# Two attention layers on one core: the first layer's products alternate between the two halves of a query block

## The chip, the cores and the metric

The kernel runs on one core of a Trainium2 chip. The metric is the device time of one execution in microseconds (us). The kernel before took 3090.68 us (median of 3 runs, 3089.88 to 3092.52).

## What is computed

The input x has 4 images of 64 x 64 tokens with 256 channels. Two attention layers follow each other. In the reference, cut to what matters:

```python
q = x @ Wq + bq; k = x @ Wk + bk; v = x @ Wv + bv          # layer 0: q, k have 32 channels, v has 256
attn = softmax(q @ k.T);  x = gamma * (attn @ v) + x       # 4096 queries x 4096 keys in each image
f = x @ Wf + bf; g = x @ Wg + bg; v = x @ Wh + bh          # layer 1: f, g have 32 channels, v has 128
beta = softmax(g @ f.T);  out = x + (beta @ v) @ Wo + bo
```

## The kernel before, in words

Nothing of size 4096 x 4096 is stored. Both layers go through blocks of queries, and within a block through steps over the keys. The first layer has blocks of 256 queries (16 in an image) and steps of 512 keys (8 in a block, each four key tiles of 128); the second has blocks of 512 queries and 16 steps of 256 keys. So each image has 128 steps of the first layer and 128 of the second; the change is in the first, in 4 x 16 = 64 blocks and 512 steps.

A step of the first layer does this:

- Scores: TensorE multiplies four key tiles with the block's queries into a PSUM tile `st` of two banks (line 640, four matmuls of 256 columns; two of them go to one bank, two to the next).
- ScalarE takes two exponentials of `st`: `high` (line 650, with a small negative bias, rounded to fp32r) and `p` (line 657, fp32).
- VectorE cuts the rest into `low` = p - high (line 678) and `d`, a combination of low and high (line 683). With three such forms of p and three of v (`v0h`, `v0l`, `v0d`), three passes of fp32r matmuls stand for one pass of higher precision.
- Products: TensorE multiplies p's forms with v's (line 708). The 128 queries of a half of the block are the stationary operand (a weight load of 128 columns per product), and v's row tile of 256 channels and two extra columns is the moving operand: 258 columns, or 256 for the l form outside a block's last step. A half has two accumulators in PSUM, one for h and l, one for d: `acc0` and `acc1` for the first half, the two banks of `acc_pair` for the second. Each is a bank of its own.

With three forms, four key tiles and two halves a step has 24 products. Call the eight products of one form in one step a section. `products_first` (line 701) issues the four products of one half and one form. The loop over the steps (from line 1039) calls it: in the inner steps of a block the order is h of half 0, h of half 1, l of half 0, l of half 1; in a block's first and last step (`s.first`, `s.last`) it is h and l of half 0, then h and l of half 1. After these come the scores of the step after next (`later.scores()`) and other small work of the plan (`todo`: projections, transposes), and then d of both halves (lines 1134 and 1135).

At a block's end `take_first` (line 744) copies a half's h and l accumulator with ScalarE to a tile `o`, as soon as that half's h and l are done, and `end_first` (line 748) adds the d accumulator with VectorE (line 752), first half first. The rest of the end (reciprocal of the sums, residual, stores) is put into later steps.

The tiles of v are allocated once, one after another (lines 366 to 374): for each of the 8 key steps the forms h, l and d, each with four rows of 260 fp32 numbers per partition (`ROW = C + 4`), 1,040 bytes a row and 4,160 bytes a tile. The forms of p are 128 x 1024 fp32 tiles; key tile g and half s begin at g x 1,024 + s x 512 bytes in a partition.

From step 8 on (`MANUAL_FROM`, line 1044) each engine executes its instructions in the order in which the program issues them. In the first 8 steps, the first block of the first image, the compiler's scheduler decides the order.

Of the kernel before, what the change touches and what calls it, by code (L numbers as in the profile page):

```python
# [57 lines left out]
P = 128  # L58
# [194 lines left out]
def fast_path(ctx: ExitStack, tc: tile.TileContext, x, w0, w1, wo, bo, gamma, out, off):  # L253

    nc = tc.nc
# [8 lines left out]
    G = (4, 2)  # L264
# [101 lines left out]
    v0 = []  # L366
# [190 lines left out]
    def project_stages(b, l, h):  # L557
        return transpose_stages(b, l, h), qk_stages(b, l, h), v_stages(b, l, h)
# [28 lines left out]
    def wide(name, until, dtype=F32):  # L587
        step = now[0] % PER_IMAGE - PER_LAYER
        until_step = until - (now[0] - now[0] % PER_IMAGE) - PER_LAYER

        def may_have(k):
            if isinstance(k, int):
                return True
            if isinstance(k, str):
                return step >= 0 and now[0] // PER_IMAGE == B - 1
            if dtype != F32R or step < 0:
                return False
            return now[0] // PER_IMAGE == B - 1 or until_step < VALUES_FROM[k[0]]

        which = min((k for k in free_at if may_have(k)), key=free_at.get)  # L600
        free_at[which] = until
        while any(held is not None and held == in_slot.get(which) for _, _, _, held in later_sums):
            later_sums.pop(0)[2]()
        in_slot[which] = name
        if isinstance(which, str):
            return const.tile([P, NT, QB0], dtype, tag=which, name=name)
        if not isinstance(which, int):
            return v0[which[0]][which[1]][:, :, :C]
        return work.tile([P, NT, QB0], dtype, tag=f"wide{which}", bufs=1, name=name)

    def small(name):
        return work.tile([P, C], F32, tag="small", bufs=4, name=name)


    class Step:
# [82 lines left out]

            later_sums.append((1.15, self.n + (KEEP if self.n < last_block else 0), issue, f"p_{self.key}"))

        def products_first(self, acc, s, what):
            p, v, which = {
                "h": (self.high, "h", 0), "l": (self.low, "l", 0), "d": (self.d, "d", 1)
            }[what]

            width = C if what == "l" and not self.last else W
            for g in range(G[0]):
                nc.tensor.matmul(  # L708
                    acc[2 * s + which][:, :width],
                    p[:, g, s * P : (s + 1) * P],  # L710
                    v0[self.i][v][:, g, :width],
                    start=self.first and what != "l" and g == 0,
                    stop=self.last and what != "h" and g == G[0] - 1,
                )

        def products_second(self, acc, parts, halves=(slice(0, QB // QB0),), between=None):
            v = v_t[self.b, self.i]
# [22 lines left out]
    def out_rows(b, j, s):  # L740
        row = j * QB0 + s * P
        return out[b, row : row + P, :]

    def take_first(b, j, acc, o, s):
        o.append(work.tile([P, W], F32, tag="o", name=f"o_{b}_{j}_{s}"))
        nc.scalar.activation(o[s], acc[2 * s][:, :W], AF.Copy, scale=1.0 + EPS)
# [175 lines left out]
    def run(stages):  # L922
        for u in stages:
            u()
# [78 lines left out]
    acc, p_sum, o = None, None, []  # L1003
# [35 lines left out]
    for n, s in enumerate(steps):  # L1039
        now[0] = n  # L1040
        b, l, j = s.b, s.l, s.j
        if n == last_block:
            tc.mark_branch_hint_location("in_range", "LikelyTaken", mybir.ALL_ENGINES)
        if n == MANUAL_FROM:
            ordered.enter_context(tc.manual_schedule())
        if s.first:
            o = []
            acc = [ps_main.tile([P, QB], F32, tag=f"acc{a}", name=f"acc{a}_{b}_{l}_{j}") for a in range(2)]
            if l == 0:
                pair = ps_main.tile([P, 2, QB], F32, tag="pair", name=f"acc_pair_{b}_{j}")  # L1050
                acc += [pair[:, a, :] for a in range(2)]
            if l == 1:
                p_sum = wide(f"p_sum_{b}_{j}", n + NI[1] + MOVED_AT + 2.5)
        if l == 0 and s.i == NI[0] - 3:
            x_res[b, j] = []
            for t in range(NS):
                x_res[b, j].append(small(f"x_res_{b}_{j}_{t}"))
                row = (j * NS + t) * P
                nc.sync.dma_start(x_res[b, j][t], x[b, row : row + P, :])
                nc.sync.dma_start(out_rows(b, j, t), bias[1, :].partition_broadcast(P))  # L1060
        if l == 0 and s.i == NI[0] - 2:
            for t in range(NS):
                nc.gpsimd.dma_start(x_res[b, j][t], bias[0, :].partition_broadcast(P), accum_op=ALU.add)

        ahead = steps[n + Q_AHEAD] if n + Q_AHEAD < len(steps) else None
        if ahead is not None and ahead.first:
            k = (ahead.b, ahead.l, ahead.j * (QB0, QB)[ahead.l] // QB)
            if k not in q_t:
                load_q(*k)
        if b == l == j == 0 and s.i == 5:  # L1070
            load_q(0, 0, 0, slice(QB0, QB), qk_dram[0, 0, 0].bitcast(F32R)[:, :, :, QB0:])
        after, later = (steps[n + k] if n + k < len(steps) else beyond for k in (1, 2))

        early = []
        if b == l == j == 0 and s.i + AHEAD < NB:
            early = [project_stages(0, 0, 2 * (s.i + AHEAD) + k) for k in range(2)]
            run([u for x in early for u in x[0]])

        run(todo.pop((n, "a"), []))
        s.move_sum()  # L1080
        if l == 0:
            s.cut_both()
            after.cut_low()
        else:
            cost = 1.9 if s.split else 2.2
            tensor_clock += cost + 1.7 * (b + 1 < B and s.i in (3, 7)) + 0.86 * (j > 0 and s.i in (13, 14))
            vector_clock = max(vector_clock, tensor_clock - cost)
            s.cut_both()
            after.cut_low()
            vector_clock += 1.15 * (s.split + after.split)  # L1090
            if n < len(steps) - 2:
                s.add_up(p_sum)
        if l == 1:
            if n == len(steps) - 2:
                while later_sums:
                    later_sums.pop(0)[2]()
                last_sums(p_sum)
            if s.last:
                o = take_first_two(b, j, acc)
            if s.first and j == 0:  # L1100
                s.products_second(acc, ("h", "l"))
            later.scores()
            run(todo.pop((n, "b"), []))

            while later_sums and (later_sums[0][1] <= n or vector_clock + later_sums[0][0] <= tensor_clock + AHEAD_OF):
                took, _, issue, _ = later_sums.pop(0)
                issue()
                vector_clock += took
            behind = steps[n - 1] if not s.first and steps[n - 1].split else None
            if s.last and behind:  # L1110
                behind.products_second(acc, ("d",))
            if n == len(steps) - 1:
                halves = [slice(k, k + 1) for k in range(QB // QB0)]
                s.products_second(acc, ("whole",), halves, last_denominators)
            elif not (s.first and j == 0):
                s.products_second(acc, ("h", "l") if s.split else ("whole",))
            if not s.last and behind:
                behind.products_second(acc, ("d",))
            if n == len(steps) - 1:
                last_outputs(acc, o)  # L1120
            elif s.last:
                vector_clock += 0.8
                end_second(b, j, acc, p_sum, o, n + 1)
        else:

            for half, what in ((0, "h"), (0, "l"), (1, "h"), (1, "l")) if s.first or s.last else ((0, "h"), (1, "h"), (0, "l"), (1, "l")):
                s.products_first(acc, half, what)
                if s.last and what == "l":
                    take_first(b, j, acc, o, half)
            if early:  # L1130
                run([u for x in early for u in x[1] + x[2]])
            later.scores()
            run(todo.pop((n, "b"), []))
            for half in (0, 1):
                s.products_first(acc, half, "d")
            if s.last:
                end_first(b, j, acc, o, n + 1)

        over = (min(s.i + 2, NI[l] - 1) + 1) * G[l] // NT if j == NQ[l] - 1 else 0
        while keys and stored.get(keys[0], n + 1) <= n and (keys[0][:2] == (b, l) or keys[0][2] < over):  # L1140
            load_k(*keys.pop(0))
# [55 lines left out]
```

## Time and profile before

| what | value |
|---|---|
| median of 3 runs | 3090.68 us |
| the profiled execution's own time | 3090.66 us |
| its span, first to last instruction | 3088.8 us |
| mean granted TensorE clock | 0.999 |
| TensorE busy | 3065.6 us (99%) |
| weight loads busy | 2668.0 us (86%) |
| VectorE busy | 2743.3 us (89%) |
| ScalarE busy | 2198.2 us (71%) |
| products of the first layer (line 708) | 12,288 |

Matmuls are pipelined, so a matmul's own length in the profile (some 280 ns for a product) overlaps its neighbours' and does not say how fast they follow each other; for that one compares the starts. "PEld" is TensorE's weight load, "PEclk" the granted clock in tenths. A line of a group reads: line, engine, operation, output <- inputs, size, count | busy us, mean ns of one | idle time of the engine ahead of it, and what ended most of that. A line of sums over a window reads: window, length, then busy us and number of instructions of TensorE, weight loads, VectorE, ScalarE and GpSimd, then the clock, the DMAs' share and GB/s.

### The profile page before, as it was taken

Reading aid. Unit: us, or ns where it says so; the run is one execution under the profiler, and the core shown is the slowest. Engines: PE = TensorE matmul, PEld = TensorE weight load, DVE = VectorE, ACT = ScalarE, POOL = GpSimd, SP = SyncE. Lnnn points to the kernel's source line nnn. Section 1 sums busy time; section 2 is a strip of 40 time slices with the busy share of each in tenths; the row PEclk is TensorE's granted clock in tenths of the full one; section 3 lists DMA queues with packets and bytes.
Section 4 is the critical chain, followed back from the end, with each engine's and each line's share of the span. In section 5 each row is a group of like instructions: output and inputs, shape, how many; then the busy total and the mean of one; then the engine's idle time right before and its main releaser. Section 6 shows DMA issues by size and latency. Waiting matters only on the chain.

```text
span 3088.8 us, 55044 instructions
## 1 busy us (share of the span) xinstructions
PE 3065.6 (99%) x19908; PEld 2668.0 (86%) x19908; DVE 2743.3 (89%) x3317; ACT 2198.2 (71%) x2900; POOL 788.9 (26%) x1157
## 2 busy tenths in 40 slices
PE   8999999999999999999999999999999999999999
PEld 7999998666799999866689999976668999997666
DVE  7889989999889999999989998999998888888887
ACT  6777777777677777777767677777776666667775
POOL 5111113222421111422241111132234111124332
PEclk9999999999999999999999999999999999999999
DMA  5344445666644444666664444466666333337877
GB/s 134 77 90 88 90 88 116 141 135 136 131 89 90 88 91 88 129 132 136 133 126 94 87 91 88 89 132 130 133 136 118 64 68 74 60 75 159 158 155 144
DMA packets 458888, 338.45 MB, mean 110 GB/s; under 512 B 266386, under 2 KB 400404, under 8 KB 458612
## 3 DMA queue, kind: packets, MB, share of 16 engines
q0 software_dynamic: 112272, 196.49, 35.4%
q1 hardware_dynamic: 345140, 137.80, 18.3%
q8 instruction: 161, 2.64, 0.4%
q14 instruction: 115, 0.94, 0.1%
q10 hardware_dynamic: 1200, 0.59, 0.1%
HBM read 134.74 MB, written 101.78 MB: 77 GB/s over the span
## 4 chain that ended last, share of the span: by engine, by line
PE 91%; DVE 4%; DMA 1%; issue 1%; ACT 1%; SPq 0%; POOL 0%; ACTq 0%; DVEq 0%; POOLq 0%
PE acc_pair L708 23%; PE acc L708 23%; PE acc L732 23%; PE st L640 14%; PE psv L509 5%; PE psqk L458 2%; PE pso L846 2%; DMA p_sum_moved<-p 1%; DVE p_sum L697 1%; DVE d L683 1%; DVE low L678 0%; ACT p L657 0%; SPq L293 0%; DVE v0l L683 0%; DVE v0h L678 0%
## 5 line engine op out<-in xcount | busy, mean ns | idle before, releaser
L650 ACT ACTIVATE high<-st,down 128x1024 fp32r<-128x1024 f32 x651 | 727.3, 1117 | 651.6 <-PE st L640 557.5
L657 ACT ACTIVATE p<-st 128x1024 f32<-128x1024 f32 x1024 | 1023.3, 1019 | 30.7 <-DMA p_sum_moved<-p 16.4
L678 DVE TENSOR_TENSOR low<-p,high 128x1024 fp32r<-128x1024 f32 x565 | 690.5, 1222 | 134.8 <-ACT p L657 130.2
L683 DVE SCALAR_TENSOR_TENSOR d<-low,high 128x1024 fp32r<-128x1024 f32 x547 | 667.5, 1220 | 14.5
L640 PE MATMUL st<-q,k 128*128 128x256 f32 (+1 forms) x3072 | 660.1, 323 | 1.9 <-ACT p L657 1.0
L640 PEld LDWEIGHTS st<-q,k 128*128 128x128 f32 x3072 | 469.0, 188 | 59.6 <-issue 13.0
L732 PE MATMUL acc<-p,v 128*128 128x512 f32 (+1 forms) x1028 | 482.5, 592 | 0.2
L708 PE MATMUL acc<-v0d,d 128*128 128x258 f32 x2048 | 336.7, 286 | 2.2 <-DVE d L683 2.0
L708 PE MATMUL acc_pair<-v0h,high 128*128 128x258 f32 x2048 | 330.2, 283 | 0.0
L708 PE MATMUL acc<-v0h,high 128*128 128x258 f32 x2048 | 330.2, 283 | 0.0
L708 PE MATMUL acc_pair<-v0d,d 128*128 128x258 f32 x2048 | 329.9, 283 | 0.0
L708 PE MATMUL acc_pair<-v0l,low 128*128 128x256 f32 (+1 forms) x2048 | 325.4, 281 | 0.0
L708 PE MATMUL acc<-v0l,low 128*128 128x256 f32 (+1 forms) x2048 | 324.9, 280 | 0.0
L773 POOL DMA_DIRECT2D out<-x x128 | 114.3, 893 | 810.7 <-DVE x L767 795.6
L732 PEld LDWEIGHTS acc<-p,v 128*128 128x128 f32 x1028 | 192.1, 189 | 143.9 <-issue 124.5
L697 DVE TENSOR_TENSOR p_sum<-p_sum,p 128x1024 f32<-128x1024 f32 x239 | 291.3, 1219 | 0.4
L708 PEld LDWEIGHTS acc<-v0d,d 128*128 128x128 f32 x2048 | 282.2, 190 | 4.9 <-DVE d L683 3.7
L671 POOL DMA_DIRECT2D p_sum_moved<-p x167 | 151.8, 913 | 517.1 <-DMA p_sum_moved<-p 196.2
L708 PEld LDWEIGHTS acc<-v0h,high 128*128 128x128 f32 x2048 | 282.4, 190 | 1.5 <-ACT o L789 0.8
L708 PEld LDWEIGHTS acc_pair<-v0h,high 128*128 128x128 f32 x2048 | 281.4, 189 | 0.3 <-DVE o L752 0.2
L708 PEld LDWEIGHTS acc_pair<-v0d,d 128*128 128x128 f32 x2048 | 280.7, 189 | 0.1
L708 PEld LDWEIGHTS acc_pair<-v0l,low 128*128 128x128 f32 x2048 | 277.3, 188 | 0.0
(181 smaller groups left out, 4281.0 us busy)
## 6 DMA issues: line engine op xcount, KB each, us to landing
p_sum_moved<-p POOLq DMA_DIRECT2D x207, 512.0 KB, 4.9
x_res<-in_x SPq DMA_DIRECT2D x128, 128.0 KB, 3.2
qk_dram<-qk_parts SPq DMA_DIRECT2D x128, 128.0 KB, 2.2
x_res<-bias POOLq DMA_DIRECT2D x128, 128.0 KB, 4.1
out<-bias SPq DMA_DIRECT2D x128, 128.0 KB, 4.2
out<-x POOLq DMA_DIRECT2D x128, 128.0 KB, 3.1
q<-qk_dram POOLq DMA_DIRECT2D x252, 64.0 KB, 3.8
out<-y POOLq DMA_DIRECT2D x124, 128.0 KB, 4.0
```

The lines of the kernel that those rows point to most:

```text
L458: nc.tensor.matmul(t["ps"], wqk[l][:, c, :], x_parts[key][n][:, c, :], start=(c == n == 0), stop=(c == NCC - 1 and n == 1),)
L509: nc.tensor.matmul(ps[:, n, :], xT[key][:, c, n * P : (n + 1) * P], wv[l][:, c, :], start=(c == 0), stop=(c == NCC - 1),)
L640: nc.tensor.matmul(st[:, g, :], k_t[b, l, kt // NT][:, kt % NT * P : (kt % NT + 1) * P], q_t[b, l, j * n // QB][:, q0 : q0 + n], start=Tru ...
L650: nc.scalar.activation(self.high, s_flat, AF.Exp, bias=down)
L657: nc.scalar.activation(self.p, s_flat, AF.Exp)
L671: nc.gpsimd.dma_start(moved_sums[b, j, order % both], self.p, accum_op=ALU.add)
L678: nc.vector.tensor_sub(self.low, self.p, self.high.bitcast(F32))
L683: nc.vector.scalar_tensor_tensor(self.d, self.low.bitcast(F32), -UP, self.high.bitcast(F32), ALU.mult, ALU.add)
L697: nc.vector.tensor_add(p_sum, other, self.p)
L708: nc.tensor.matmul(acc[2 * s + which][:, :width], p[:, g, s * P : (s + 1) * P], v0[self.i][v][:, g, :width], start=self.first and what != ...
L732: nc.tensor.matmul(acc[which].rearrange("p (a n) -> p a n", n=QB0)[:, cols, :], v_part[:, g, :], p[:, g * NS : (g + 1) * NS, :][:, cols, : ...
L773: nc.gpsimd.dma_start(out_rows(b, j, s), x_new, accum_op=ALU.add)
```

## The change

`products_first` takes the halves as a list and loops over them inside the loop over the key tiles. In the inner steps of a block h and l are issued for both halves together, so that the products of the two halves alternate for each key tile; d is issued so in all steps. In a block's first and last step h and l keep their order. The line numbers after line 708 grow by one.

```diff
-        def products_first(self, acc, s, what):
+        def products_first(self, acc, halves, what):
...
             for g in range(G[0]):
-                nc.tensor.matmul(
-                    acc[2 * s + which][:, :width],
-                    p[:, g, s * P : (s + 1) * P],
-                    v0[self.i][v][:, g, :width],
-                    start=self.first and what != "l" and g == 0,
-                    stop=self.last and what != "h" and g == G[0] - 1,
-                )
+                for s in halves:
+                    nc.tensor.matmul(
+                        acc[2 * s + which][:, :width],
+                        p[:, g, s * P : (s + 1) * P],
+                        v0[self.i][v][:, g, :width],
+                        start=self.first and what != "l" and g == 0,
+                        stop=self.last and what != "h" and g == G[0] - 1,
+                    )
...
-            for half, what in ((0, "h"), (0, "l"), (1, "h"), (1, "l")) if s.first or s.last else ((0, "h"), (1, "h"), (0, "l"), (1, "l")):
-                s.products_first(acc, half, what)
+            ends = s.first or s.last
+            for halves, what in (((0,), "h"), ((0,), "l"), ((1,), "h"), ((1,), "l")) if ends else (((0, 1), "h"), ((0, 1), "l")):
+                s.products_first(acc, halves, what)
                 if s.last and what == "l":
-                    take_first(b, j, acc, o, half)
+                    take_first(b, j, acc, o, halves[0])
...
-            for half in (0, 1):
-                s.products_first(acc, half, "d")
+            s.products_first(acc, (0, 1), "d")
```

## Prediction, made before the changed kernel ran

> **What bounds the kernel now.** I read the page first (busy times, the clock row, the chain), then the timeline of TensorE over one step of the first layer, then the sums over whole blocks of queries, then the waits of the tile `o`.
>
> ```profile
> PE 3065.6 (99%) x19908; PEld 2668.0 (86%) x19908; DVE 2743.3 (89%) x3317; ACT 2198.2 (71%) x2900; POOL 788.9 (26%) x1157
> ...
> PEclk9999999999999999999999999999999999999999
> ...
> PE acc_pair L708 23%; PE acc L708 23%; PE acc L732 23%; PE st L640 14%; PE psv L509 5%; PE psqk L458 2%; PE pso L846 2%; DMA p_sum_moved<-p 1%; DVE p_sum L697 1%; DVE d L683 1%; DVE low L678 0%; ACT p L657 0%; SPq L293 0%; DVE v0l L683 0%; DVE v0h L678 0%
> ...
> L708 PE MATMUL acc<-v0d,d 128*128 128x258 f32 x2048 | 336.7, 286 | 2.2 <-DVE d L683 2.0
> L708 PE MATMUL acc_pair<-v0h,high 128*128 128x258 f32 x2048 | 330.2, 283 | 0.0
> ```
>
> TensorE is busy 99% at full clock, 46% of the chain is line 708, and those products wait for next to nothing (the idle column: 0.0 to 2.2 us). Three whole blocks (256 queries, 8 key steps each) say it again:
>
> ```profile
> 993.07:1021.59 28.52, 28.52 (x242) 28.52 (x241) 26.14 (x35) 20.21 (x28) 3.48 (x4) 1.00 0.45 84
> 1021.59:1050.11 28.52, 28.52 (x242) 28.52 (x241) 25.48 (x33) 20.20 (x28) 5.55 (x8) 1.00 0.48 96
> 1050.11:1078.63 28.52, 28.52 (x242) 28.52 (x241) 26.14 (x35) 20.20 (x28) 3.48 (x4) 1.00 0.45 84
> ```
>
> Every block takes 28.52 us, whatever VectorE (fourth figure: 26.14 or 25.48 us) and the DMAs do. So the first layer's time is the sum of the distances from one matmul's start to the next one's, and a change of order is worth what it does to these distances. A row's mean (283 ns) is no help: matmuls overlap. One step in the timeline (start, length, engine, line):
>
> ```profile
> 1028.69 0.64 PE L708 MATMUL acc_pair<-v0d,d 128*128 128x258 f32 x4
> 1029.17 0.64 PE L708 MATMUL acc<-v0h,high 128*128 128x258 f32 x4
> 1029.65 0.64 PE L708 MATMUL acc_pair<-v0h,high 128*128 128x258 f32 x4
> 1030.13 0.63 PE L708 MATMUL acc<-v0l,low 128*128 128x256 f32 x4
> 1030.60 0.63 PE L708 MATMUL acc_pair<-v0l,low 128*128 128x256 f32 x4
> 1031.06 0.64 PE L640 MATMUL st<-q,k 128*128 128x256 f32 x4
> ```
>
> From start to start four products take 0.48 us (258 columns) or 0.46 to 0.47 (256): 120 and 117 ns each.
>
> **The change, part by part.** Nothing is added or removed: the same products, weight loads and operands. The built programs' order is the same on ScalarE, GpSimd and SyncE, with every DMA in its place. On TensorE the products of a section (one of h, l, d in one step: 4 key tiles x 2 halves) go 0,1,0,1,... where they went 0,0,0,0,1,1,1,1. That holds for d in all 512 steps (4,096 products) and for h and l in the 6 inner steps of 8 (384 x 16 = 6,144): 10,240 products.
>
> *Distance of one product.* I took the starts of the trace one by one (after 100 us, distances over 140 ns left out). They depend on the place in the block and on hardly anything else: 11,001 distances between products have a variance of 10.0 ns2, of which 1.3 is left once the product's moving operand and the weights loaded next to it are fixed (addresses modulo 2,048). They run from 114 to 130 ns and repeat: at key steps 1 and 5 the third product of h's second half takes 129.9 and 130.0 ns, that of its first half 119.2 and 119.2. These steps' tiles of v are 4 x 3 x 4,160 = 49,920 bytes apart, a multiple of 256. So the place of the moving operand modulo 256 bytes, and what went before, set the distance. Under the change each product keeps its moving operand. The weights loaded beside it are other ones (512 bytes on, not 1,024), but as all these starts differ by multiples of 512 the places modulo 256 stay the same set. If the place decides, the mean stays: 119.2 ns over the 80 places concerned (h and l: 6 steps x 4 key tiles each, d: 8 x 4; 119.0 first half, 119.4 second). Gain or loss: 0.
>
> *Bounds.* At one place the two halves differ, by 3.3 ns on average. If both took the shorter, the mean would fall by 1.63 ns; if the longer, rise by 1.63: 10,240 x 1.63 = 16.7 us either way. Between these I take 0, the row's own mean. The scatter: there are 12 kinds of section (three forms, four places), whose means have a standard deviation of 1.1 ns; a fresh draw of 12 against the old one moves the mean by 1.1 x sqrt(2/12) = 0.46 ns, 4.7 us.
>
> *What the Trainium skill says.* "TensorE: Matmul & The Clock Gate", section "Back-to-back issue gap", gives columns / 2.4 + 2.5 ns: 110.0 ns for 258 columns. By that every order costs the same, the change is worth nothing, and 9 ns of each product are unexplained. The row is 119.2 and varies with the place, so order can matter; the rows decide, and the page is no reason for a narrow range. The same page, "A second HAM failure mode: psum-queue depth-cycling", speaks against the change: cycling through PSUM banks made TensorE fall back to half clock now and then. At 258 / 1.2 = 215 ns, 10,240 products would cost 980 us more. But the scores (L640) change banks every second matmul already, the products every fourth, and the clock is 1.00 in all three blocks: I cost it at 0.
>
> *End of a block.* Here the first half's d sum is complete later: before, four products ahead of the second's, now one, so 3 x 0.12 = 0.36 us later. VectorE adds both to `o` (L752):
>
> ```profile
> 1021.38 0.42 DVE L752 TENSOR_TENSOR o<-o,acc 128x258 f32<-128x258 f32 x1 [1.00 <-PE acc L708]
> ...
> 1021.87 0.42 DVE L752 TENSOR_TENSOR o<-o,acc_pair 128x258 f32<-128x258 f32 x1
> ...
> 1022.21 1.22 DVE L683 SCALAR_TENSOR_TENSOR d<-low,high 128x1024 fp32r<-128x1024 f32 x1
> ...
> 1024.76 0.54 PEld L708 LDWEIGHTS acc<-v0d,d 128*128 128x128 f32 x4
> ```
>
> The first add starts at 1021.74 and the second follows it, 1022.23 instead of 1021.87. Queued behind are L683's d, 0.3 to 0.4 us later (done near 1023.8), and the next low. TensorE wants that d at 1024.76: the 1.34 us between 1023.42 and there shrink to about 1.0. The same 1.34 stands at nearly all of the other ends inside the layer (0.43 at each image's first, once per image). VectorE idles 1.0 us at each end, so the delay doesn't add up. Cost 0; with this cover gone, up to 64 x 0.36 = 23 us. In the four switches to the second layer an add also frees a bank for scores: at most 4 x 0.36 = 1.4 us, taken as 0.
>
> *New waits.* The second half's first d product comes 0.36 us sooner and needs its bank emptied by L752, done at 1022.3 (now 1022.65) against 1024.9. No wait. In the first image's first block end, where the order is not by hand, VectorE now has one d ahead of the two adds; 0.43 us of cover stand against at most 1 us of loss, once. I take 0.
>
> Sum: 3090.66 (the profiled execution: span 3088.8 and 1.9 around it; the median of the runs is 3090.68) + 0 = 3091.
>
> **The rivals.** *Faster: changing accumulators pays.* Distances that lead to the other accumulator average 118.9 ns against 120.2 that stay (258 columns), 116.6 against 118.1 (256): 1.4 ns less. Each section has one such change inside now and would have 7: 6 x 1,280 sections x 1.4 ns = 10.8 us, 3080. Against it: of these changes, those from d to the next h average 120.6, no better than staying; and on the scores, which stay, change, stay, the three distances are 117.7, 117.7 and 119.2. Few places lie behind the 1.4.
>
> *Slower: the repeated read costs.* Two products in a row now read the same v, with weights 512 bytes apart. Only the scores do just that (same q, k tiles 512 bytes apart, 256 columns): 118.2 ns on average against 117.7 for l, +0.5 ns, 5 us. If instead both halves fall into the longer distance of their place, 16.7 us. Between these I price the case at 1 ns, 10 us: 3101. It decides the sign from a mean distance of 119.8 on (0.6 x 10,240 = 6 us). For it: the longest distances (130 ns) are near their worst already in one half only, and a place is now used twice running.
>
> *No effect at all*, the order being undone on the chip: matmuls start in the order written in this trace, so I give it no share apart from the first case.
>
> **How the numbers follow.** No shift, 3091: 0.40. Faster by the accumulators, 3080: 0.26. Slower by the repeated read, 3101: 0.32. Clock or the block's end after all, beyond 3104: 0.02. A measurement tells about 0.2% (6.2 us) from no change. With 4.7 us of scatter the first case gives 0.34 within that and 0.03 on each side; the second 0.22 faster, 0.04 within; the third 0.26 slower, 0.06 within. Faster 0.25, same 0.44, slower 0.31. The range reaches to a little beyond the two rivals' values: 3078 to 3104. The likeliest case's own range is 3085 to 3097.
>
> **What would show it.** A block is 28.52 us: at 0 shift it stays within 0.08; by the first rival it is 28.3, by the second 28.7. Eight alternating products should take 0.96 us from start to start, single distances still between 114 and 130 and repeating with key step + 4. The waits of L752 grow by about 0.36 us each (now 60.0 us in all), with no wait of TensorE for d behind it. I am wrong if the distances leave that band or lose their pattern, if the clock row drops under 9, or if products begin to wait for L683 or L752.

## The result and the profile after

The changed kernel takes 3103.01 us (median of 6 runs, 3099.68 to 3104.70) against 3091.73 us (6 runs, 3089.88 to 3093.51): a ratio of 1.0037, 95% interval 1.0026 to 1.0048. It is slower by 0.4%, some 11.3 us. The profiled execution took 3101.95 us with a span of 3100.2 us; the one of before took 3090.66 us with 3088.8, so the traces differ by 11.4 us of span and stand for the medians.

The page of the kernel after, with the rows that answer to those of before, and the row of one weight load:

```profile
PE 3076.2 (99%) x19908; PEld 2675.6 (86%) x19908; DVE 2735.9 (88%) x3317; ACT 2200.5 (71%) x2900; POOL 791.1 (26%) x1157
...
PEclk9999999999999999999999999999999999999999
...
L709 PE MATMUL acc<-v0d,d 128*128 128x258 f32 x2048 | 518.9, 285 | 1.8 <-DVE d L683 1.7
...
L709 PE MATMUL acc_pair<-v0h,high 128*128 128x258 f32 x2048 | 474.4, 286 | 0.8 <-DVE o L753 0.8
...
L709 PEld LDWEIGHTS acc_pair<-v0h,high 128*128 128x128 f32 x2048 | 361.6, 190 | 4.2 <-DVE o L753 1.2
```

The same weight loads on the page of before:

```profile
L708 PEld LDWEIGHTS acc_pair<-v0h,high 128*128 128x128 f32 x2048 | 281.4, 189 | 0.3 <-DVE o L752 0.2
```

Two traps lie in these rows. First, the busy time of `acc_pair<-v0h` grew from 330.2 to 474.4 us, and no product became that much slower: busy time is the union of overlapping lengths, and products of one group that alternate with another group's overlap each other less. Second, the idle time of these products is 0.8 us, which looks like nothing. What tells more is the releaser named there, `o L753`, and the idle time of the weight loads ahead of them: 0.3 us before, 4.2 us after. The weight loads' row of before names the same releaser already, with 0.2 us.

Sums over three whole blocks (window, length, then busy us and instructions of TensorE, weight loads, VectorE, ScalarE and GpSimd, clock, DMA share, GB/s):

```profile
997.91:1026.56 28.65, 28.65 (x243) 28.60 (x242) 26.00 (x35) 20.23 (x28) 3.49 (x4) 1.00 0.44 84
1026.56:1055.21 28.65, 28.65 (x243) 28.60 (x242) 25.32 (x33) 20.21 (x28) 5.56 (x8) 1.00 0.49 96
1055.21:1083.87 28.66, 28.66 (x243) 28.61 (x242) 25.99 (x35) 20.23 (x28) 3.49 (x4) 1.00 0.43 84
```

A block takes 28.65 us instead of 28.52, again the same in every block, at clock 1.00. That is +0.13 to 0.14 us for each of 64 blocks, 9 us in all. Taken from the starts of the trace, the first layer grew from 1851.70 to 1861.34 us (first to last product of each image, the four summed): 9.64 of the 11.4 us. The weight loads now fill 28.60 us of a window where they filled 28.52 of 28.52: each block has 0.05 us in which none runs. So somewhere in the block something waits. The block's end in the timeline (start, length, engine, line), first before, where the second add to `o` starts at 1021.87 and ends at 1022.29:

```profile
1022.44 0.55 PEld L708 LDWEIGHTS acc_pair<-v0h,high 128*128 128x128 f32 x4
1022.55 0.65 PE L708 MATMUL acc_pair<-v0h,high 128*128 128x258 f32 x4
```

And after:

```profile
1026.56 0.42 DVE L753 TENSOR_TENSOR o<-o,acc 128x258 f32<-128x258 f32 x1 [1.36 <-PE acc L709]
...
1026.90 0.42 DVE L753 TENSOR_TENSOR o<-o,acc_pair 128x258 f32<-128x258 f32 x1
1027.23 1.22 DVE L683 SCALAR_TENSOR_TENSOR d<-low,high 128x1024 fp32r<-128x1024 f32 x1
...
1027.37 0.54 PEld L709 LDWEIGHTS acc_pair<-v0h,high 128*128 128x128 f32 x4
1027.37 0.75 PE L709 MATMUL acc_pair<-v0h,high 128*128 128x258 f32 x4
...
1027.95 0.63 PE L709 MATMUL acc_pair<-v0l,low 128*128 128x256 f32 x4
```

Before, the weights of half 1's first product in the next block are loaded 0.11 us ahead of its start (1022.44, then 1022.55), 0.15 us after the second add has ended. After, the add ends at 1027.32 and the load and the product both start at 1027.37: they were held by it, and the load no longer lies beside the product before. The group of four is 0.75 us long where it was 0.65. The product that follows comes 223 ns after the first instead of 119 (medians over the blocks): 0.104 us a block. A product's modelled length is some 283 ns and covers a distance of 223, so the profile shows almost no idle time of TensorE.

### The profile page after: what moved, and what is told of

Its sections match the earlier page's. It is cut to its first block, busy times and chain, and to the rows that moved or that the text cites. A ratio compares the mean times of both kernels' runs of the same rounds, so it can differ in the third digit from the quotient of the medians.

```text
span 3100.2 us, 55045 instructions
## 1 busy us (share of the span) xinstructions
PE 3076.2 (99%) x19908; PEld 2675.6 (86%) x19908; DVE 2735.9 (88%) x3317; ACT 2200.5 (71%) x2900; POOL 791.1 (26%) x1157
## 4 chain that ended last, share of the span: by engine, by line
PE 93%; DVE 4%; DMA 1%; issue 1%; ACT 1%; SPq 0%; POOL 0%; DVEq 0%; POOLq 0%; ACTq 0%
PE acc L733 23%; PE acc_pair L709 23%; PE acc L709 23%; PE st L640 15%; PE psv L509 5%; PE pso L847 2%; PE psqk L458 2%; DVE p_sum L697 1%; DVE d L683 0%; DVE low L678 0%; DMA p_sum_moved<-p 0%; SPq L293 0%; DVE v0h L678 0%; DVE qk_parts L485 0%; DMA q<-qk_dram 0%
## 5 line engine op out<-in xcount | busy, mean ns | idle before, releaser
L709 PE MATMUL acc<-v0d,d 128*128 128x258 f32 x2048 | 518.9, 285 | 1.8 <-DVE d L683 1.7
L709 PE MATMUL acc_pair<-v0d,d 128*128 128x258 f32 x2048 | 513.0, 283 | 0.0
L709 PE MATMUL acc_pair<-v0h,high 128*128 128x258 f32 x2048 | 474.4, 286 | 0.8 <-DVE o L753 0.8
L709 PE MATMUL acc<-v0h,high 128*128 128x258 f32 x2048 | 469.3, 284 | 0.0
L709 PE MATMUL acc<-v0l,low 128*128 128x256 f32 (+1 forms) x2048 | 463.9, 281 | 0.0
L709 PE MATMUL acc_pair<-v0l,low 128*128 128x256 f32 (+1 forms) x2048 | 462.4, 281 | 0.0
L709 PEld LDWEIGHTS acc<-v0d,d 128*128 128x128 f32 x2048 | 389.4, 190 | 4.0 <-DVE d L683 2.9
L709 PEld LDWEIGHTS acc_pair<-v0d,d 128*128 128x128 f32 x2048 | 387.4, 189 | 0.6
L709 PEld LDWEIGHTS acc<-v0l,low 128*128 128x128 f32 x2048 | 359.6, 189 | 0.0
L709 PEld LDWEIGHTS acc_pair<-v0l,low 128*128 128x128 f32 x2048 | 359.1, 188 | 0.0
```

The source lines that it names most:

```text
L709: nc.tensor.matmul(acc[2 * s + which][:, :width], p[:, g, s * P : (s + 1) * P], v0[self.i][v][:, g, :width], start=self.first and what != ...
```

## The experiments

The theories, as the expectations name them. W: half 1's first h product waits for the second add to `o`, since the two banks of `acc_pair` are one tile, and the alternating d of a block's last step completes half 0 later and so delays both adds. R: the repeated read of the same v costs, wherever products alternate. P: the place of v against the weights in memory decides, and the order only draws other places. Block times are medians over the first three images, from the starts of the one profiled execution of each kernel; before has 28.520 us and after 28.660.

**Only the last step's d as before, or only that changed.** These two split the change in two. The first, on the kernel after:

```diff
-            s.products_first(acc, (0, 1), "d")
+            for halves in (((0,), (1,)) if s.last else ((0, 1),)):
+                s.products_first(acc, halves, "d")
```

> As the changed kernel, but in a block's last step d keeps its old order (half 0, then half 1). Theory W (a wait): two thirds of the loss is a wait at each block's start, where the first h product of half 1 needs the tile acc_pair, which the second add to o frees 0.1 us too late; 61 x 0.104 us and 0.94 us once. Then a block takes 28.55 us instead of 28.65 and the kernel about 3096 us. Theory R (the repeated read of v makes the products slow, and nothing else): 7 of 8 steps still repeat, so about 3102 us and 28.64 us a block.

The second keeps the old order of h, l and d everywhere but for d in a block's last step:

```diff
+            for halves in (((0, 1),) if s.last else ((0,), (1,))):
+                s.products_first(acc, halves, "d")
```

> As the kernel before, but in a block's last step d alternates. Theory W: the whole wait is here: about 28.62 us a block (28.52 + 0.104) and 3099 us. Theory R: only 512 of the 10,240 products repeat: 28.53 us a block and 3092 us, no change.

The weight loads of half 1's h on the page of the first, then on the page of the second:

```profile
L709 PEld LDWEIGHTS acc_pair<-v0h,high 128*128 128x128 f32 x2048 | 362.9, 190 | 0.3 <-DVE o L753 0.2
```

```profile
L709 PEld LDWEIGHTS acc_pair<-v0h,high 128*128 128x128 f32 x2048 | 280.7, 190 | 4.2 <-DVE o L753 1.2
```

The idle time of 4.2 us follows the last step's d alone. With it as before, a block is 28.553 us and the kernel 3093.80 us (before on the same chip 3090.91; 1.0010, 1.0003 to 1.0017). With only it changed, 28.620 us and 3099.32 us (1.0029, 1.0018 to 1.0041). So the 512 products at block ends (eight at each of 64), of 10,240 with a changed place, carry 0.100 us of the block's 0.140; everything else in the change carries 0.033.

**Same order of products, the other add first.** On the kernel after, in `end_first`:

```diff
-        for s in range(NS):
+        for s in reversed(range(NS)):
```

> As the changed kernel, with all its alternation, but VectorE adds half 1 to o first, so that acc_pair is free 0.33 us earlier; acc1 is needed only three microseconds later. Theory W: no wait, 28.55 us a block and about 3096 us. Theory R: as the changed kernel, 28.65 us and 3103 us.

The block's end in its timeline:

```profile
1024.48 0.42 DVE L753 TENSOR_TENSOR o<-o,acc_pair 128x258 f32<-128x258 f32 x1 [1.48 <-PE acc_pair L709]
...
1024.82 0.42 DVE L753 TENSOR_TENSOR o<-o,acc 128x258 f32<-128x258 f32 x1
...
1025.05 0.55 PEld L709 LDWEIGHTS acc_pair<-v0h,high 128*128 128x128 f32 x4
...
1025.16 0.65 PE L709 MATMUL acc_pair<-v0h,high 128*128 128x258 f32 x4
```

Here the add that reads `acc_pair` comes first: VectorE waits 1.48 us for the products that it adds, longer than for the first add after the change, and yet it ends at 1024.90, 0.15 us ahead of the load. The load leads its product by 0.11 us again, the group is 0.65 us long, the distance is 120 ns, and the block takes 28.540 us. TensorE's order is that of the kernel after, so the wait was the add and not the order of products. The first layer takes 7.8 us less than after, 7.4 of them in the distances around half 1's first h product. The kernel takes 3096.48 us, 1.0020 of before (1.0010 to 1.0029) where after took 1.0037. But that is 5.6 us over before, of which the first layer has only 1.85 (1853.55 against 1851.70).

**Alternating without repeating v.** From here on the question is the small rest: what alternating itself does to the distances. On the kernel with the other add first, half 1 takes its key tiles two, one or three further on, so that neighbours no longer read the same v:

```diff
+                    gs = (g + 2 * s) % G[0] if len(halves) > 1 else g
...
-                        p[:, g, s * P : (s + 1) * P],
-                        v0[self.i][v][:, g, :width],
+                        p[:, gs, s * P : (s + 1) * P],
+                        v0[self.i][v][:, gs, :width],
```

> As the kernel that adds half 1 first, but half 1 runs two key tiles behind half 0: the accumulators still alternate, no two products in a row read the same v. Theory R: what the wait does not explain (0.03 to 0.04 us a block) goes: 28.52 us a block and 3092 us. Theory P (the distance of a product is set by the place of its operands, so every order is a fresh draw): the block differs from that kernel's 28.55 us by up to 0.05 us either way, single distances again between 114 and 130 ns.

> Half 1 added to o first, halves alternating, half 1 one key tile ahead: 3 of the 7 steps inside a section read the v of the product just before. Theory R (a repeated read of v costs): 3/4 of the way from the two-tiles-apart kernel (28.493 us a block) to the straight alternation (28.540, where 4 of 7 repeat): about 28.53 us. Theory P (the place decides, each order is a fresh draw): anything from 28.45 to 28.58 us, section by section unlike both.

> The same with half 1 three key tiles ahead: no repeated read of v, accumulators alternate. Theory R: as two tiles apart, 28.49 us a block. Theory P: anything from 28.45 to 28.58 us. If alternating accumulators by itself helped, this one and the last would both lie below the 28.52 us of before.

| order of an alternating section | block, us | first layer, us | span of the profiled execution, us |
|---|---|---|---|
| same tile (v read twice running) | 28.540 | 1853.55 | 3094.3 |
| half 1 two tiles on | 28.493 | 1851.61 | 3090.9 |
| half 1 one tile on | 28.527 | 1854.36 | 3093.6 |
| half 1 three tiles on | 28.560 | 1856.35 | 3094.5 |
| halves in turn (before) | 28.520 | 1851.70 | 3088.8 |

R falls as the cause: three tiles apart reads no v twice running and is the slowest of the four. A cost of the repeated read that is small against the 0.067 us between these orders isn't excluded. That a change of accumulator pays falls too, since all four change it at every product and lie on both sides of before. Two tiles apart was also timed: 3093.74 us against 3090.91 (1.0010, 1.0003 to 1.0017), not faster as a whole although its blocks are.

**Moving the operands in memory, nothing else.** Three kernels on the order of before. In one, v's tiles of the last key step are allocated first, so that each step's v lies where the next step's lay:

```diff
-    v0 = []
-    for j in range(NB):
+    v0 = [None] * NB
+    for j in (NB - 1, *range(NB - 1)):
...
-        v0.append(forms)
+        v0[j] = forms
```

> The kernel before, order of products untouched; the tiles of v of key step 7 are allocated first, so that each step's v lies where the next step's lay. Theory P: a section's time moves along with the place: h of steps 1 to 6 takes 955, 959, 956, 963, 955, 959 ns for its eight products (before 963, 955, 959, 956, 963, 955), l takes 937, 944, 943, 942, 937, 944 (before 942, 937, 944, 943, 942, 937); the block stays within 0.02 us of 28.52. If the position in the block or the order decides instead, the sections keep their times.

In the next a tile of 32 bytes a partition, allocated after v and written once at the start, moves p and all that follows by 32 bytes; in the third the same tile is allocated ahead of v and moves v and p together:

```diff
+    nc.vector.memset(const.tile([P, 8], F32, name="gap"), 0.0)
```

> The kernel before, order untouched, 32 unused bytes a partition allocated after v, so that p's forms lie 32 bytes further on against v. Theory P: a fresh draw at the same set of places: sections change by up to 20 ns each, the block stays within 0.1 us of 28.52. If the operands' places don't matter, sections and block are those of before (28.52).

> The kernel before, order untouched, 32 unused bytes a partition allocated ahead of v, so that v and p both lie 32 bytes further on. If only the place of v against the weights counts, sections and block are those of before: h 963, 955, 959, 956, 963, 955 ns, 28.52 us. If the place of v by itself counts, they change by up to 20 ns a section, as when p alone was moved.

Time from the start of one section of h to the start of the next section, eight products, in ns (medians):

| kernel | step 1 | step 2 | step 3 | step 4 | step 5 | step 6 |
|---|---|---|---|---|---|---|
| before | 963 | 955 | 959 | 956 | 963 | 955 |
| v one step on | 955 | 959 | 952 | 963 | 955 | 959 |
| p 32 bytes on | 958 | 953 | 967 | 964 | 958 | 953 |
| v and p 32 bytes on | 963 | 955 | 959 | 952 | 963 | 955 |
| after (alternating) | 967 | 973 | 951 | 959 | 956 | 973 |

With v one step on, the row of before moves one step to the left, within 4 ns. With p alone 32 bytes on, four of the six sections change by 5 to 8 ns and the other two by 2. With both moved, the row of before comes back, again within 4 ns. Work and order are those of before in all three, so what counts is where v lies against the weights. The blocks take 28.507, 28.467 and 28.527 us, the last within 0.01 of before; the spans are 3088.8, 3086.0 and 3089.3 us (before 3088.8).

**The change at the other places.** The 32 bytes of p, now on the alternating kernel with the other add first:

> The kernel with all the alternation and half 1 added first, and p's forms 32 bytes further on against v, as in the run before. Theory P: a new draw, between 28.40 and 28.58 us a block. Theory R or any cost of the alternation by itself: above the 28.467 us that the old order takes at these places, by the 0.02 us or more that it was above the old order at the first places.

One add per block end in the timeline of VectorE, for p moved in the old order, then for p moved and alternating:

```profile
991.10 0.42 DVE L753 TENSOR_TENSOR o<-o,acc 128x258 f32<-128x258 f32 x1 [0.99 <-PE acc L709]
...
1019.57 0.42 DVE L753 TENSOR_TENSOR o<-o,acc 128x258 f32<-128x258 f32 x1 [0.99 <-PE acc L709]
```

```profile
996.65 0.42 DVE L754 TENSOR_TENSOR o<-o,acc_pair 128x258 f32<-128x258 f32 x1 [1.47 <-PE acc_pair L710]
...
1025.21 0.42 DVE L754 TENSOR_TENSOR o<-o,acc_pair 128x258 f32<-128x258 f32 x1 [1.46 <-PE acc_pair L710]
```

From one block to the next these are 28.47 and 28.56 us (28.467 and 28.567 over the blocks). At these places alternating costs 0.100 us a block, at the first ones 0.020 (28.540 against 28.520). The same edit of the order has another price once p lies 32 bytes further on; the kernel took 3099.64 us in its one run.

**An order chosen section by section.** On the alternating kernel with the other add first, each section takes the order that was shortest for it in the runs above: by key step, `None` is halves in turn, a number is how many key tiles half 1 is ahead.

```diff
+    turns = {
+        "h": (0, 2, None, 0, None, 2, None, 0),
+        "l": (0, None, None, 2, 0, None, None, 0),
+        "d": (0, 0, 1, 2, 2, 1, 1, 2),
+    }
```

> Half 1 added to o first; each section (form and key step) takes the one of five orders measured so far that was the fastest for it: halves in turn, alternating, or half 1 one or two key tiles apart. Theory P, if sections keep their times beside other neighbours: h of steps 1 to 6 takes 948, 955, 951, 956, 948, 955 ns, l 942, 937, 942, 934, 942, 937; against before a block saves 0.139 us: 28.38 us, and the kernel 8.9 us: about 3082 us, faster than both. If what a section takes depends on the sections around it, the sum fails: 28.45 to 28.55 us.

The block took 28.480 us, not the 28.38 that the sum of the sections promised, and the kernel 3092.67 us against 3091.42 (1.0003, 0.9995 to 1.0012). h came out in steps 2, 4, 5 and 6 as in the runs that it was taken from (957, 957, 948 and 956 ns against 955, 956, 948 and 955), but took 975 in step 1 instead of 948 and 960 in step 3 instead of 951, and d took 972 in step 2 instead of 948. What stands beside a section matters there, which the first two runs had not shown: their sections were those of before or after one by one. So P, each section by itself, is not the whole rule.

**The best version, timed.** The order of before with p 32 bytes on, now over 13 runs:

> The kernel before, order untouched, with 32 unused bytes between v and p's forms, as looked at once already (28.467 us a block, 0.053 less than before), now timed against the kernel before. If the block's gain reaches the whole: 64 x 0.053 = 3.4 us, about 3088 us (0.9989). If the second layer gives it back: no difference.

Its blocks take again 28.467 us, the first layer 1848.48 us, 3.2 less than before. The kernel takes 3089.26 us against 3090.66: 0.9994, 0.9986 to 1.0002. Its blocks are the shortest seen, but as a whole it can't be told from before.

## Why the prediction held in its range and was wrong in its mechanism

It put 3091 us as the likeliest and no measurable change as the likeliest outcome. That 3103 lies in its range of 3078 to 3104 is luck: the range reached so far up for the repeated read, and what came was a wait that it had put at nothing. By its own sign, products that begin to wait for L752, it was wrong. By its steps:

- **The distance of one product: right in size, not in its reason.** In the inner steps the means moved from 119.8 to 120.4 ns (h), from 117.8 to 118.7 (l) and from 120.0 to 119.6 (d), by these means 2 to 3 us over the whole layer (1.9 in the account below) against a forecast of 0 with 4.7 of scatter. The distances stayed between 112 and 130 ns and repeated with key step + 4. After as before, the moving operand and the next weights, by their places, leave hardly any of the variance (2.0 of 11.1 ns²). The runs that moved v and p show that the place decides, but not v's place modulo 256 bytes by itself: with v and p both 32 bytes on that place was another one and the distances stayed. What counts is the place relative to the weights. And that the sum came so near 0 is in part the luck of the places: with p 32 bytes on, the alternation costs 0.100 us a block, 6.4 us over 64 blocks. An alternating section in the timeline of after, forecast at 0.96 us for eight products, takes 31.71 - 30.74 = 0.97:

```profile
1030.74 0.28 PE L709 MATMUL acc<-v0h,high 128*128 128x258 f32 x1
1030.87 0.28 PE L709 MATMUL acc_pair<-v0h,high 128*128 128x258 f32 x1
...
1031.71 0.29 PE L709 MATMUL acc<-v0l,low 128*128 128x256 f32 x1
```

- **The two rules of the Trainium skill: rightly set behind the rows.** From the formula in "TensorE: Matmul & The Clock Gate", "Back-to-back issue gap", an estimate is 110.0 ns; the traces have 112 to 130 by place, before and after. The page calls this formula the gap of an isolated matmul and not that of a stream of weight loads and matmuls, which the prediction left out. The half clock of "A second HAM failure mode: psum-queue depth-cycling" did not come with a change of bank at every product: 0.999, as before.
- **The end of a block: right for the first add and for d.** The first add's wait grew from 1.00 to 1.36 us, the forecast 0.36. Over the blocks, in the waits view (releaser, us in all, count, longest), before and after:

```profile
DVE o L752 <- PE acc L708: 60.0, 59, 1.5
```

```profile
DVE o L753 <- PE acc L709: 86.1, 63, 2.0
```

  The second add was not pushed back as far as forecast: it starts 0.49 us after the block's first product (1026.90 against 1026.41) where it started 0.27 after it (1021.87 against 1021.60), and it ends 0.21 us later, not 0.36 (also the median over 59 blocks). Before, it had waited for its own products and came 0.49 us after the first add; now it follows at 0.34. The cover of d behind the adds is 1.23 us here (done at 1028.45, loaded at 1029.68). TensorE's waits for d did not grow: 2.0 us in 4 before, 1.7 in 3 after.
- **"New waits": the step that failed.** It asked who needs the emptied bank and named "the second half's first d product", with over 2 us to spare. But that is the third form of the half. Its first product in the new block is h, 0.96 us after the block's start, and writes the other bank of the same tile `acc_pair`. Yet h waits for the add that reads the d bank: after the change its load starts 0.05 us behind that add's end at all of the 59 block ends inside the layer that follow the first. So the program releases the tile as a whole. In the trace of before 0.15 us lie between that add's end and h's load (1022.29, 1022.44), so with these 0.05 us only 0.10 were to spare. The add's end came 0.21 us later, and h's load 0.11. The second h product then comes 0.104 us later (median), at 59 block ends more than before: 6.2 us in the sum of the distances. The prediction's own push of 0.36 us would have given 0.26. The trace of before even holds this wait once, in one of its last blocks, where the second add came 0.36 us later than elsewhere:

```profile
2659.04 0.42 DVE L752 TENSOR_TENSOR o<-o,acc_pair 128x258 f32<-128x258 f32 x1 [0.42 <-PE acc_pair L708]
...
2659.51 0.54 PEld L708 LDWEIGHTS acc_pair<-v0h,high 128*128 128x128 f32 x4 [0.19 <-DVE o L752]
2659.51 0.75 PE L708 MATMUL acc_pair<-v0h,high 128*128 128x258 f32 x4
```

  The load starts with its product, the group is 0.75 us long, and the distances before and after the first h product are 268 and 230 ns instead of 116 and 119: 0.26 us lost. This is the 0.2 us of `o L752` in the weight loads' row of before; it named who waits for whom before the change was made.
- **The first block's end, taken at 0: wrong, and small.** There the compiler put one d ahead of both adds, and half 1's first h product waits, once:

```profile
90.77 0.42 DVE L753 TENSOR_TENSOR o<-o,acc_pair 128x258 f32<-128x258 f32 x1
...
91.25 0.39 PE L709 MATMUL acc_pair<-v0h,high 128*128 128x258 f32 x1 [0.77 <-DVE o L753]
```

  The prediction's "at most 1 us" was the right size: the distance there is 1,050 ns where it was 118.
- **The rival that came near in time was wrong in its cause.** "The repeated read costs" said 3101 and a block of 28.7; the time was 3103 and the block 28.66. Nothing in R made it: with the wait away, the repeated read's block is 28.540, between those of orders that repeat nothing.

The account, after minus before: the distances around half 1's first h product give 7.8 us of the first layer's 9.64 (6.2 the wait at 59 block ends, 0.9 more at the first of them, the rest around them), all other distances 1.9 us. The remaining 1.7 of 11.4 us of span lie outside the first layer, where nothing was changed.

**What stays open.** Outside the first layer the traces differ from 1237.1 to 1241.7 us (before 1237.1, after 1238.8); why the kernel with the other add first and the one with p moved and alternating are 3.7 and 4.7 us above before there was not found. Why the second add came late once in the trace of before is open too. Why the relative place of v and the weights sets the distance isn't shown, nor why neighbours counted in the order chosen by section. That two tiles of one bank each in place of `acc_pair` would do away with the wait was not tried.

## What to carry to other kernels

When a change delays an instruction, list everything that waits for any part of the tile it reads, in the order in which the next round issues it, and compare the first one's start with the delayed end: the slack is read from the starts and ends, since the waits show only slack that has run out. But a releaser that a row names even once, with 0.2 us, says who waits for whom, and is worth looking up. A wait shorter than a matmul's modelled length is all but invisible as idle time of TensorE; look for a weight load that starts with its product, a longer group, and the distance of the starts. And before a change of order is judged by some tenths of a per cent, move an operand by a few bytes: if that alone does as much, the order was not what was measured.

## What was not expected of the hardware

- 32 bytes in the place of the weights changed the block of about 240 matmuls from 28.520 to 28.467 us, and the price of the same reordering from 0.020 to 0.100 us a block. Moving both operands by the same 32 bytes left it at 28.527.
- Changing the accumulator at each product has no fixed price: blocks of 28.493 to 28.560 us in four orders that all do so, around 28.520 for the one that changes every fourth.
- A delay of 104 ns was not made good: the products behind it kept distances of some 119 ns, and with the wait away the block was 0.107 to 0.120 us shorter.
